# Row sums of the attention weights moved from TensorE to GpSimd, and a third PSUM bank in the ring of a two-layer graph network

## The chip, the cores and the metric

The kernel runs on one core of a Trainium2 chip. The metric is the device time of one execution in microseconds; the median of several runs is given. A profiled execution adds a trace of every instruction; its span runs from the first to the last instruction. The engines are called PE (TensorE), PEld (its weight loads), DVE (VectorE), ACT (ScalarE), POOL (GpSimd) and SP (SyncE, which issues most DMAs).

## The reference

The input `x` is (16, 1024, 256) in fp32, the adjacency `adj` (16, 1024, 1024) in int32. Two layers follow, each with a normalisation and a ReLU ahead of it and a residual around it:

```python
h = relu(layernorm(x))
# layer 0, 8 heads of 32
n = layer_norm(h, gamma1, beta1)                      # queries, keys and values are all n
s = einsum('bhqd,bhkd->bhqk', n, n) / sqrt(32)
attn = softmax(where(adj > 0, s, -inf), axis=-1)
h1 = h + einsum('bhqk,bhkd->bhqd', attn, n)
x = x + h1 + gelu(layer_norm(h1, gamma2, beta2) @ W1 + b1) @ W2 + b2
# layer 1, one head of 256
f = relu(layernorm(x))
h = f @ W
e = leaky_relu((h @ a_1).T + h @ a_2 + (h @ a_12) @ h.T, 0.2)
att = softmax(where(adj > 0, e, -9e15), axis=-1)
x = x + elu(f @ W_1 + (att @ f) @ W_2)
```

The change concerns the softmax of layer 0: its denominators, the sums of the exponentials over the keys.

## The kernel before, in words

The program holds two paths, chosen on the chip from `gamma1` and `beta1`; with these inputs `fast_path` runs. It works batch by batch (`B` = 16). In a batch, layer 0's attention is cut into 32 units: two halves of 512 queries (`qh`), two groups of four heads (`g`), eight tiles of 128 keys (`kt`). Eight units that share `qh` and `g` make a group, and there are 64 groups in all.

A unit first computes its scores (`scores`, L734): four matmuls with a contraction of 32, one for each head, into one tile `sc` of four PSUM banks (L739); the tile has one buffer only. Keys lie on the partitions, queries along the free dimension. DVE adds the mask to two heads at a time and writes an SBUF tile `e` of 128 x 1024 (L750, twice for each unit), and ACT takes the exponential in place (L751). The pool `ep` has four such tiles, two units' worth. No maximum is subtracted in this path.

`weigh` (L759) comes one unit later in PE's order, after the scores of the next unit. It has two rounds of four narrow matmuls (L770), one for each head, 32 output partitions each: the first adds exponentials times values into the bank `o`, the second multiplies the same exponentials with a tile of ones and adds up `den`, the row sums, repeated over the 32 partitions of each head. Both accumulate over the eight key tiles in the two banks of the pool `pso`. At the last key tile DVE copies `o` and ACT copies `den` to SBUF (L782). `finish` (L715) turns both by PE transposes (L721), and DVE divides (L724, L726); POOL adds the result to `h` (L728).

An fp32 matmul is two instructions for the engine, so that the profile shows 4096 where the program has 2048.

Everything else in a batch belongs to other streams: `prologue` (L663) normalises the next batch's `x`, makes the values `va` and the transposed keys `kT`; `turn_masks` (L697) loads and transposes masks; `rest` (L807) does the batch's feed-forward part (`expand`, `contract`) and layer 1 (`project`, `values`, `logits`, `soften`, `turn_weights`, `attend`). Their PE output goes through one ring of PSUM banks, the tag `ps` in the pool `psm` (L547), with two banks before. POOL does small work: the reciprocal roots of the normalisations (L652), on whose result DVE's normalising (L656) waits, the scaling of the values (L686, L687), bias and residual additions (L822, L823, L1000).

The order of the work is written by hand: each stream yields places on one scale (units of a batch), and the main loop (L1119 to L1123) always advances the stream with the lowest place. `stream_a` spreads the 32 units evenly over a batch; `stream_b` starts `rest` at 0.95 of the batch and places its pieces by their cost in microseconds, divided by `B_US` = 151. PE keeps the order in which the program issues (L1126 to L1138). On the other engines a scheduler orders the instructions. Each engine works through its own queue in order, and waits at an instruction until what it needs is done.

Of the kernel before, what the change touches and what calls it, by code (L numbers as in the profile page):

```python
# [9 lines left out]
F32 = mybir.dt.float32  # L10
# [5 lines left out]
P = 128  # L16
# [470 lines left out]
def fast_path(  # L487
# [26 lines left out]
    nc = tc.nc  # L514
    B, N, D = x.shape
    DFF = W1.shape[1]
    H, HD = 8, D // 8
    GH = 4
    NG = H // GH
    NT = N // P  # L520
    DC = D // P
    FC = DFF // P
    QW = 512
# [7 lines left out]
    pool = lambda name, bufs, **kw: ctx.enter_context(tc.tile_pool(name=name, bufs=bufs, **kw))  # L531
# [7 lines left out]
    vp = pool("vp", 2)  # L539
    midp = pool("midp", 3)  # L540
    ep = pool("ep", 4)
    lp1 = pool("lp1", 2)
    tmpp = pool("tmpp", 2)
    smallp = pool("smallp", 3)
    psc = pool("psc", 1, space=bass.MemoryType.PSUM)
    pso = pool("pso", 1, space=bass.MemoryType.PSUM)
    psm = pool("psm", 2, space=bass.MemoryType.PSUM)  # L547

    def ps_tile(shape, name, dtype=F32):
        return psm.tile(shape, dtype, tag="ps", name=name)  # L550
# [16 lines left out]
    ones = const.tile([P, HD], F32, name="ones")  # L567
# [29 lines left out]
    w2 = weight(W2, "w2")  # L597
# [112 lines left out]

    scored, summed = [], []

    def finish(b, qh, g, cs):  # L715
        h = hs[b]
        pts = []
        for n, c in cs:
            pt = ps_tile([P, TPH, P], f"pt{n}_{b}_{g}_{qh}")
            for t in range(TPH):  # L720
                nc.tensor.transpose(pt[:, t, :], c[:, t * P : (t + 1) * P], ident)  # L721
            pts.append(pt.rearrange("p t (j d) -> p t j d", d=HD))
        rl = smallp.tile([P, TPH, GH], F32, tag="rl", name=f"rl_{b}_{g}_{qh}")
        nc.vector.reciprocal(rl, pts[0][:, :, :, 0])  # L724
        ot = tmpp.tile([P, TPH, GH, HD], F32, tag="w2", bufs=3, name=f"ot_{b}_{g}_{qh}")
        nc.vector.tensor_mul(ot, pts[1], rl.unsqueeze(3).to_broadcast([P, TPH, GH, HD]))  # L726
        ho = h[:, qh * TPH : (qh + 1) * TPH, g * P : (g + 1) * P]
        nc.gpsimd.tensor_add(ho, ho, ot.rearrange("p t j d -> p t (j d)"))  # L728

    def attention(b, st):  # L730
        va, kT = st["va"], st["kT"]


        def scores(qh, g, kt):  # L734
            qs = slice(qh * QW, (qh + 1) * QW)
            sc = psc.tile([P, GH, QW], F32, tag="sc", name=f"s_{b}_{g}_{qh}_{kt}")
            for j in range(GH):
                r = slice(j * HD, (j + 1) * HD)
                nc.tensor.matmul(  # L739
                    sc[:, j, :],  # L740
                    kT[r, g, kt * P : (kt + 1) * P],
                    kT[r, g, qs],
                    start=True,
                    stop=True,
                )
            mb = st[qh][:, kt, :].unsqueeze(1).to_broadcast([P, 2, QW])
            es = []
            for i in range(2):
                e = ep.tile([P, 2, QW], F32, tag="e", name=f"e_{b}_{g}_{qh}_{kt}_{i}")
                nc.vector.tensor_tensor(e, sc[:, 2 * i : 2 * i + 2, :], mb, op=ALU.add)  # L750
                nc.scalar.activation(e, e, AF.Exp, scale=SCALE)  # L751
                es.append(e)
            return es

        acc = {}

        def weigh(qh, g, kt, es):  # L759
            if kt == 0:  # L760
                acc[g, qh] = [
                    pso.tile([P, QW], F32, tag=n, name=f"{n}_{b}_{g}_{qh}") for n in ("o", "den")
                ]
            o, den = acc[g, qh]
            for dst, lhs in (
                (o, [va[:, kt, (g * GH + j) * HD : (g * GH + j + 1) * HD] for j in range(GH)]),
                (den, [ones] * GH),
            ):
                for j in range(GH):
                    nc.tensor.matmul(  # L770
                        dst[j * HD : (j + 1) * HD, :],
                        lhs[j],
                        es[j // 2][:, j % 2, :],
                        start=(kt == 0),
                        stop=(kt == NT - 1),
                    )
            if kt < NT - 1:
                return
            cs = []
            for src, n in ((den, "ds"), (o, "os")):  # L780
                c = tmpp.tile([P, QW], F32, tag="w2", bufs=3, name=f"{n}_{b}_{g}_{qh}")
                (nc.vector.tensor_copy if n == "os" else nc.scalar.copy)(c, src)  # L782
                cs.append((n, c))
            summed.append((b, qh, g, cs))

        units = [(qh, g, kt) for qh in range(NQH) for g in range(NG) for kt in range(NT)]
        for u in units:
            es = scores(*u)
            while summed:
                finish(*summed.pop())  # L790
            while scored:
                f, args = scored.pop()
                f(*args)
            scored.append((weigh, (*u, es)))
            yield

    def close_attention():
        while scored:
            f, args = scored.pop()
            f(*args)  # L800
        yield
        while summed:
            finish(*summed.pop())

    def rest(b, tail):  # L807
# [8 lines left out]
        def prepare(c):  # L816
            ts = range(c * TPC, (c + 1) * TPC)
            mv, rs = norm_stats([h[:, t, :] for t in ts], f"c{b}_{c}")
            y = tmpp.tile([P, TPC, D], F32, tag="y", name=f"y_{b}_{c}")
            for i, t in enumerate(ts):  # L820
                normalize(y[:, i, :], h[:, t, :], mv, rs, i)
                nc.gpsimd.tensor_add(h[:, t, :], h[:, t, :], b2r)  # L822
                nc.gpsimd.tensor_add(xt[t], xt[t], h[:, t, :])  # L823
            return y
# [20 lines left out]
        def expand(c, yT):  # L845
            hid = midp.tile([P, FC, CW], F32, tag="mid", name=f"hid_{b}_{c}")
            for f0 in range(0, FC, 2):
                ph = ps_tile([P, 2, CW], f"ph_{b}_{c}_{f0}")
                for i in range(2):
                    for dc in range(DC):  # L850
                        nc.tensor.matmul(  # L851
                            ph[:, i, :],
                            w1[:, dc, (f0 + i) * P : (f0 + i + 1) * P],
                            yT[:, dc, :],
                            start=(dc == 0),
                            stop=(dc == DC - 1),
                        )
                nc.vector.tensor_tensor(  # L858
                    hid[:, f0 : f0 + 2, :],
                    ph,  # L860
                    b1c[:, f0 : f0 + 2].unsqueeze(2).to_broadcast([P, 2, CW]),
                    op=ALU.add,
                )
                yield 1.75, True
            nc.scalar.activation(hid, hid, AF.Gelu)
            return hid
# [136 lines left out]
        y = {0: prepare(0), 1: prepare(1)}  # L1003
# [1 line left out]
        yT = {0: turn(0, y[0])}  # L1005
        yield 0.5, True
        hid = {0: (yield from expand(0, yT[0]))}
        y[2] = prepare(2)
        yT[1] = turn(1, y[1])
        yield 0.5, True  # L1010
        yield from tail()
        hid[1] = yield from expand(1, yT[1])
        y[3] = prepare(3)
        yT[2] = turn(2, y[2])
# [52 lines left out]
        def tail():  # L1067
            pTs = [turn_weights(before[0], before[1], i) for i in range(2)]
            yield 0.9, True
            attend(before[0], pTs, before[2])  # L1070
            yield 4.4, True
# [6 lines left out]
    def spread(pieces, n, start, end):  # L1078
        yield start
        for i, _ in enumerate(pieces):  # L1080
            yield start + (end - start) * (i + 1) / n
# [3 lines left out]
    def stream_a():  # L1085
        for b in range(B):
            yield from spread(attention(b, states[b]), 32, b, b + 1)
        yield from spread(close_attention(), 2, B, B + 0.05)

    def stream_b():  # L1090
        tail = lambda: iter(())
        for b in range(B):
            done = 0.0
            place = b + 0.95
            yield place
            pieces = rest(b, tail)
            while True:
                try:
                    us, others = next(pieces)
                except StopIteration as end:  # L1100
                    tail = end.value
                    break
                done += us
                if others:
                    place = b + 1 + done / B_US
                yield place
        for _ in tail():
            yield B + 1
# [12 lines left out]
    while any(p is not None for p in places):  # L1121
        i = min((p, i) for i, p in enumerate(places) if p is not None)[1]
# [77 lines left out]
```

## Time and profile before

| what | before |
|---|---|
| median of 3 runs | 4816.01 us (4811.63 to 4816.24) |
| the profiled execution | 4813.6 us |
| its span | 4811.4 us |
| mean granted TensorE clock | 0.969 |
| until the first mask addition (L750) starts | 62.8 us |
| one batch between the first and the last | about 297 us |
| DMA | 192.14 MB, 12 to 13% of 16 engines |

The page lists for each engine the busy time, its share of the span, and the number of instructions. A row of a group has line, engine, operation, what is written and read, shapes and count; behind the bar stand busy time and the mean of one in ns, then the idle time of the engine just before and what ended it. Where narrow matmuls run side by side, the mean is that of one, and the busy time counts overlaps once. A row of the waits has the waiting instruction, the one it waited for, the total in us, the number of times, and the longest. A row of the timeline has the start in us, the length, engine, line and operation.

### The profile page before, as it was taken

Reading aid. Unit: us, or ns where it says so; the run is one execution under the profiler, and the core shown is the slowest. Engines: PE = TensorE matmul, PEld = TensorE weight load, DVE = VectorE, ACT = ScalarE, POOL = GpSimd, SP = SyncE. Lnnn points to the kernel's source line nnn. Section 1 sums busy time; section 2 is a strip of 40 time slices with the busy share of each in tenths; the row PEclk is TensorE's granted clock in tenths of the full one; section 3 lists DMA queues with packets and bytes.
Section 4 is the critical chain, followed back from the end, with each engine's and each line's share of the span. In section 5 each row is a group of like instructions: output and inputs, shape, how many; then the busy total and the mean of one; then the engine's idle time right before and its main releaser. Section 6 shows DMA issues by size and latency. Waiting matters only on the chain. (4 is left out here: it accounts for less than half of the span.)

```text
span 4811.4 us, 61168 instructions
## 1 busy us (share of the span) xinstructions
PE 4273.0 (89%) x24104; PEld 2316.0 (48%) x24104; DVE 2814.2 (58%) x5329; ACT 2249.5 (47%) x2941; POOL 773.0 (16%) x969
## 2 busy tenths in 40 slices
PE   5898988989899898998989989899898988989998
PEld 2354544545445454454545445454454544545456
DVE  5656655556566565665655656555565565656553
ACT  3544445444454444444444444444444444444533
POOL 3102121021210212112121121211212111021110
PEclk8999999999999999999999999999999999999999
DMA  3011111111101111011111111101111011110100
GB/s 102 27 38 46 36 42 34 44 44 32 46 29 49 40 38 40 29 50 43 39 36 34 47 44 38 37 30 47 44 38 44 23 49 42 38 42 26 37 27 27
DMA packets 133259, 192.14 MB, mean 40 GB/s; under 512 B 15586, under 2 KB 67172, under 8 KB 132964
## 3 DMA queue, kind: packets, MB, share of 16 engines
q1 hardware_dynamic: 128004, 184.60, 12.2%
q8 instruction: 192, 3.15, 0.3%
q10 hardware_dynamic: 4960, 3.55, 0.3%
q14 instruction: 103, 0.84, 0.1%
HBM read 171.32 MB, written 16.78 MB: 39 GB/s over the span
## 5 line engine op out<-in xcount | busy, mean ns | idle before, releaser
L751 ACT ACTIVATE e<-e 128x1024 f32<-128x1024 f32 x1024 | 1080.2, 1057 | 1280.0 <-DVE e L750 1255.2
L750 DVE TENSOR_TENSOR e<-s,mk 128x1024 f32<-128x1024 f32 x1024 | 1203.2, 1215 | 294.5 <-PE s L739 288.8
L739 PE MATMUL s<-kT 32*128 32x512 f32 x4096 | 598.8, 654 | 76.0 <-DVE e L750 76.0
L936 PE MATMUL lg<-fT,tT 128*128 128x512 f32 x1024 | 499.2, 631 | 109.0 <-DVE rl L724 56.5
L770 PE MATMUL o<-e,va 128*32 128x512 f32 x4096 | 567.9, 611 | 0.8 <-ACT e L751 0.7
L770 PE MATMUL den<-e,ones 128*32 128x512 f32 x4096 | 552.4, 595 | 0.0
L986 PE MATMUL pa<-gw,pT 128*128 128x256 f32 x2048 | 493.7, 396 | 26.8 <-ACT mk L709 25.8
L851 PE MATMUL ph<-yT,w 128*128 128x256 f32 x2048 | 479.9, 385 | 14.7 <-DVE yT L835 11.8
L873 PE MATMUL po<-w,hid 128*128 128x256 f32 x2048 | 467.4, 383 | 7.1 <-DVE hid L858 5.6
L986 PEld LDWEIGHTS pa<-gw,pT 128*128 128x128 f32 x2048 | 402.7, 198 | 102.7 <-ACT mk L709 34.2
L851 PEld LDWEIGHTS ph<-yT,w 128*128 128x128 f32 x2048 | 377.2, 190 | 133.2 <-issue 24.3
L873 PEld LDWEIGHTS po<-w,hid 128*128 128x128 f32 x2048 | 381.5, 190 | 98.1 <-issue 17.4
L949 DVE CUSTOM_DVE_ANT_0 e<-e,mqb 128x1024 f32<-128x1024 f32 x128 | 158.2, 1236 | 445.3 <-ACT e L943 445.2
L936 PEld LDWEIGHTS lg<-fT,tT 128*128 128x128 f32 x1024 | 193.5, 198 | 377.1 <-issue 217.9
L739 PEld LDWEIGHTS s<-kT 32*128 32x128 f32 x4096 | 167.1, 188 | 272.9 <-issue 239.4
L770 PEld LDWEIGHTS den<-e,ones 128*32 128x32 f32 x4096 | 137.1, 111 | 310.8 <-issue 310.5
L967 PE MATMUL ptp<-ident,e 128*128 128x128 f32 x1024 | 170.9, 297 | 129.0 <-ACT e L943 102.5
L858 DVE TENSOR_TENSOR hid<-ph,b1c 128x512 f32<-128x512 f32 x256 | 176.2, 688 | 171.6 <-PE ph L851 171.5
L943 ACT ACTIVATE e<-lg,gw 128x512 f32<-128x512 f32 x256 | 171.9, 683 | 200.3 <-PE lg L936 200.3
L770 PEld LDWEIGHTS o<-e,va 128*32 128x32 f32 x4096 | 83.6, 108 | 375.1 <-issue 285.3
L728 POOL TENSOR_TENSOR h<-h,ot 128x512 f32<-128x512 f32 x64 | 82.7, 1292 | 1043.8 <-DVE ot L726 907.7
L959 ACT ACTIVATE e<-e,m 128x1024 f32<-128x1024 f32 x128 | 147.0, 1149 | 195.1 <-DVE m L957 195.0
(109 smaller groups left out, 4409.0 us busy)
## 6 DMA issues: line engine op xcount, KB each, us to landing
adj_mqa<-in_adj_dram SPq DMA_DIRECT2D x256, 256.0 KB, 2.9
adj_mqb<-in_adj_dram SPq DMA_DIRECT2D x256, 256.0 KB, 2.8
xa<-in_x_dram SPq DMA_DIRECT2D x64, 256.0 KB, 2.7
xb<-in_x_dram SPq DMA_DIRECT2D x128, 128.0 KB, 2.2
out_dram<-z SPq DMA_DIRECT2D x128, 128.0 KB, 1.7
w<-in_L_gnn_W_dram ACTq DMA_DIRECT2D x2, 1024.0 KB, 9.4
wo<-in_L_gnn_W_dram ACTq DMA_DIRECT2D x2, 256.0 KB, 4.8
wl<-in_L_gnn_W_dram ACTq DMA_DIRECT2D x1, 256.0 KB
```

The lines of the kernel that those rows point to most:

```text
L739: nc.tensor.matmul(sc[:, j, :], kT[r, g, kt * P : (kt + 1) * P], kT[r, g, qs], start=True, stop=True,)
L750: nc.vector.tensor_tensor(e, sc[:, 2 * i : 2 * i + 2, :], mb, op=ALU.add)
L751: nc.scalar.activation(e, e, AF.Exp, scale=SCALE)
L770: nc.tensor.matmul(dst[j * HD : (j + 1) * HD, :], lhs[j], es[j // 2][:, j % 2, :], start=(kt == 0), stop=(kt == NT - 1),)
L851: nc.tensor.matmul(ph[:, i, :], w1[:, dc, (f0 + i) * P : (f0 + i + 1) * P], yT[:, dc, :], start=(dc == 0), stop=(dc == DC - 1),)
L858: nc.vector.tensor_tensor(hid[:, f0 : f0 + 2, :], ph, b1c[:, f0 : f0 + 2].unsqueeze(2).to_broadcast([P, 2, CW]), op=ALU.add,)
L873: nc.tensor.matmul(po, hid[:, f, i * P : (i + 1) * P], w2[:, f, :], start=(f == 0), stop=(f == FC - 1),)
L936: nc.tensor.matmul(lg, tT[:, dc, t * P : (t + 1) * P], fT[:, dc, c * QW : (c + 1) * QW], start=(dc == 0), stop=(dc == DC - 1),)
L943: nc.scalar.activation(e[:, c * QW : (c + 1) * QW], lg, AF.Identity, bias=gw[:, t, D : D + 1])
L949: nc.vector.tensor_tensor_reduce(e, e, mq, 1.0, -3.0e38, op0=ALU.add, op1=ALU.max, accum_out=m1[:, 0:1])
L967: nc.tensor.transpose(pt[:, i, :], e[:, k * P : (k + 1) * P], ident)
L986: nc.tensor.matmul(pa, pTs[kt // TPH][:, kt % TPH, :], gw[:, kt, :D], start=(kt == 0), stop=(kt == NT - 1),)
```

## The change

The row sums are no longer a matmul at every key tile. `add_up` adds the exponentials of the key tiles on POOL into two SBUF tiles `acc` of 128 x 1024 (new pool `accp`, one buffer for each): at `kt` = 0 it only keeps the tiles, at `kt` = 1 it adds the first two, later it adds to `acc`. That makes two additions of 128 x 1024 in seven of eight units. `total` then does one round of four matmuls with the ones for each group, on the sums, into a bank of the ring `ps`, and ACT copies it out. `pso` keeps one bank (`o`), and `psm` gets a third.

`go_on` runs once for each unit: it finishes one group, totals another, weighs the unit before. A group's end is therefore spread over three units instead of two, `close_attention` has three pieces, `prepare(2)` of `rest` is moved behind the tail of the batch before, and batch 0 has a piece of 5.3 us in the place of the missing tail, which moves its places alone.

```diff
--- before.py
+++ after.py
@@ -539,12 +539,13 @@
     vp = pool("vp", 2)
     midp = pool("midp", 3)
     ep = pool("ep", 4)
+    accp = pool("accp", 1)
     lp1 = pool("lp1", 2)
     tmpp = pool("tmpp", 2)
     smallp = pool("smallp", 3)
     psc = pool("psc", 1, space=bass.MemoryType.PSUM)
     pso = pool("pso", 1, space=bass.MemoryType.PSUM)
-    psm = pool("psm", 2, space=bass.MemoryType.PSUM)
+    psm = pool("psm", 3, space=bass.MemoryType.PSUM)
 
     def ps_tile(shape, name, dtype=F32):
         return psm.tile(shape, dtype, tag="ps", name=name)
@@ -710,12 +711,23 @@
 
 
 
-    scored, summed = [], []
-
-    def finish(b, qh, g, cs):
+    scored, weighed, totalled = [], [], []
+
+    def total(b, qh, g, os, acc):
+
+        den = ps_tile([P, QW], f"den_{b}_{g}_{qh}")
+        for j in range(GH):
+            nc.tensor.matmul(
+                den[j * HD : (j + 1) * HD, :], ones, acc[j // 2][:, j % 2, :], start=True, stop=True
+            )
+        ds = tmpp.tile([P, QW], F32, tag="w2", bufs=3, name=f"ds_{b}_{g}_{qh}")
+        nc.scalar.copy(ds, den)
+        totalled.append((b, qh, g, ds, os))
+
+    def finish(b, qh, g, ds, os):
         h = hs[b]
         pts = []
-        for n, c in cs:
+        for n, c in (("ds", ds), ("os", os)):
             pt = ps_tile([P, TPH, P], f"pt{n}_{b}_{g}_{qh}")
             for t in range(TPH):
                 nc.tensor.transpose(pt[:, t, :], c[:, t * P : (t + 1) * P], ident)
@@ -755,52 +767,59 @@
         acc = {}
 
 
-
         def weigh(qh, g, kt, es):
             if kt == 0:
-                acc[g, qh] = [
-                    pso.tile([P, QW], F32, tag=n, name=f"{n}_{b}_{g}_{qh}") for n in ("o", "den")
+                acc[g, qh] = pso.tile([P, QW], F32, tag="o", name=f"o_{b}_{g}_{qh}")
+            o = acc[g, qh]
+            for j in range(GH):
+                nc.tensor.matmul(
+                    o[j * HD : (j + 1) * HD, :],
+                    va[:, kt, (g * GH + j) * HD : (g * GH + j + 1) * HD],
+                    es[j // 2][:, j % 2, :],
+                    start=(kt == 0),
+                    stop=(kt == NT - 1),
+                )
+            if kt == NT - 1:
+                c = tmpp.tile([P, QW], F32, tag="w2", bufs=3, name=f"os_{b}_{g}_{qh}")
+                nc.vector.tensor_copy(c, o)
+                weighed.append((b, qh, g, c, sums.pop((g, qh))))
+
+        sums, first = {}, {}
+
+
+        def add_up(qh, g, kt, es):
+            if kt == 0:
+                first[g, qh] = es
+                return
+            if kt == 1:
+                sums[g, qh] = [
+                    accp.tile([P, 2, QW], F32, tag=f"acc{i}", name=f"acc_{b}_{g}_{qh}_{i}")
+                    for i in range(2)
                 ]
-            o, den = acc[g, qh]
-            for dst, lhs in (
-                (o, [va[:, kt, (g * GH + j) * HD : (g * GH + j + 1) * HD] for j in range(GH)]),
-                (den, [ones] * GH),
-            ):
-                for j in range(GH):
-                    nc.tensor.matmul(
-                        dst[j * HD : (j + 1) * HD, :],
-                        lhs[j],
-                        es[j // 2][:, j % 2, :],
-                        start=(kt == 0),
-                        stop=(kt == NT - 1),
-                    )
-            if kt < NT - 1:
-                return
-            cs = []
-            for src, n in ((den, "ds"), (o, "os")):
-                c = tmpp.tile([P, QW], F32, tag="w2", bufs=3, name=f"{n}_{b}_{g}_{qh}")
-                (nc.vector.tensor_copy if n == "os" else nc.scalar.copy)(c, src)
-                cs.append((n, c))
-            summed.append((b, qh, g, cs))
+            for i, a in enumerate(sums[g, qh]):
+                nc.gpsimd.tensor_add(a, first[g, qh][i] if kt == 1 else a, es[i])
 
         units = [(qh, g, kt) for qh in range(NQH) for g in range(NG) for kt in range(NT)]
         for u in units:
             es = scores(*u)
-            while summed:
-                finish(*summed.pop())
-            while scored:
-                f, args = scored.pop()
-                f(*args)
+            go_on()
             scored.append((weigh, (*u, es)))
+            add_up(*u, es)
             yield
 
-    def close_attention():
-        while scored:
+    def go_on():
+        if totalled:
+            finish(*totalled.pop())
+        if weighed:
+            total(*weighed.pop())
+        if scored:
             f, args = scored.pop()
             f(*args)
-        yield
-        while summed:
-            finish(*summed.pop())
+
+    def close_attention():
+        for _ in range(3):
+            go_on()
+            yield
 
 
 
@@ -1005,10 +1024,10 @@
         yT = {0: turn(0, y[0])}
         yield 0.5, True
         hid = {0: (yield from expand(0, yT[0]))}
-        y[2] = prepare(2)
         yT[1] = turn(1, y[1])
         yield 0.5, True
         yield from tail()
+        y[2] = prepare(2)
         hid[1] = yield from expand(1, yT[1])
         y[3] = prepare(3)
         yT[2] = turn(2, y[2])
@@ -1085,10 +1104,10 @@
     def stream_a():
         for b in range(B):
             yield from spread(attention(b, states[b]), 32, b, b + 1)
-        yield from spread(close_attention(), 2, B, B + 0.05)
+        yield from spread(close_attention(), 3, B, B + 0.05)
 
     def stream_b():
-        tail = lambda: iter(())
+        tail = lambda: iter([(5.3, True)])
         for b in range(B):
             done = 0.0
             place = b + 0.95
```

## The prediction

> **What bounds the kernel now.** I read the page first: busy times, the slices, the groups of instructions.
>
> ```profile
> PE 4273.0 (89%) x24104; PEld 2316.0 (48%) x24104; DVE 2814.2 (58%) x5329; ACT 2249.5 (47%) x2941; POOL 773.0 (16%) x969
> ...
> PE   5898988989899898998989989899898988989998
> ...
> L750 DVE TENSOR_TENSOR e<-s,mk 128x1024 f32<-128x1024 f32 x1024 | 1203.2, 1215 | 294.5 <-PE s L739 288.8
> ...
> L770 PE MATMUL o<-e,va 128*32 128x512 f32 x4096 | 567.9, 611 | 0.8 <-ACT e L751 0.7
> L770 PE MATMUL den<-e,ones 128*32 128x512 f32 x4096 | 552.4, 595 | 0.0
> ```
>
> TensorE (PE) is busy 89%, in every slice alike; the others have room. The two L770 rows are the weighted sum `o` and the row sum `den`: 1024 rounds of four narrow matmuls each, two rounds per unit (a unit is one head group, half the queries, one key tile; 16 x 32 = 512 units). PE's idle time is 4811.4 - 4273.0 = 538 us; PE's waits, longest first, tell where:
>
> ```profile
> PE ptp L967 <- ACT e L943: 102.5, 110, 4.6
> PE s L739 <- DVE e L750: 76.0, 80, 4.7
> PE lg L936 <- DVE rl L724: 56.5, 28, 2.3
> PE lg L936 <- ACT kT L694: 51.0, 28, 2.5
> PE pg L923 <- ACT fT L898: 43.0, 28, 3.6
> PE pf L976 <- ACT kT L694: 37.1, 14, 3.0
> ```
>
> Most are not data: `lg` doesn't use `rl` or `kT`. They are waits for one of the two banks of the ring `ps`, until its last reader is done. Added up over the list, such waits are some 340 us. Only 76 us are waits for the mask addition on VectorE (DVE).
>
> What a round of `den` costs is read from the timeline of PE, one unit:
>
> ```profile
> 2026.16 1.06 PE L770 MATMUL o<-e,va 128*32 128x512 f32 x8
> 2027.04 1.04 PE L770 MATMUL den<-e,ones 128*32 128x512 f32 x8
> 2028.02 0.66 PE L831 MATMUL pty<-ident,y 128*128 128x128 f32 x4
> ```
>
> `den` starts 0.88 us after `o` (median of all such pairs 0.88), the next work 0.97 us after `den`. Bars overlap, so a unit without `den` is 0.88 us shorter, not 1.04.
>
> [...] A stretch of the timeline:
>
> ```profile
> 3080.58 1.32 DVE L949 CUSTOM_DVE_ANT_0 e<-e,mqb 128x1024 f32<-128x1024 f32 x1 [0.35 <-ACT e L943]
> 3080.89 1.59 POOL L823 TENSOR_TENSOR xb<-xb,h 128x256 f32<-128x256 f32 x1
> ...
> 3081.94 1.62 DVE L953 SCALAR_TENSOR_TENSOR e<-e 128x1024 f32<-128x1024 f32 x1
> ...
> 3082.44 1.70 POOL L822 TENSOR_TENSOR h<-h,b2r 128x256 f32<-128x256 f32 x1
> ```
>
> L823 takes 0.73 us by median, here 1.59: it ends after L949. L953 takes 1.22 alone, here 1.62: it waits for L823. L822 then waits for L953. They alternate, one whole instruction each. By class, DVE operations that start under a busy POOL: L559 421 ns becomes 1353, L999 424 becomes 836, L953 1224 becomes 1632. L750 reads one input from PSUM, and stays at 1216 against 1209: free of the lock.
>
> [...] Here 256 elements take 0.73 us (L1000) and 512 take 1.265 (L728); [...] the slope of the two rows of this trace gives the same.
>
> [...] eight matmuls of 592 ns fill 1.04 us. [...] The pools held 4 (scores) + 2 (`o`, `den`) + 2 (ring); now 4 + 1 + 3.
>
> **The change part by part.**
>
> *`den` leaves PE.* 512 x 0.88 = 451 us removed; one sum per group comes back, 64 x 0.97 = 62. PE gains 388 us, all on the engine that sets the end.
>
> *Third bank.* Of the 340 us of bank waits I take 200: a wait for the tile two back becomes one for the tile three back, with one more PE tile (1 to 2 us) of cover, against mean waits of 0.9 to 2.7 us. Bounds 100 and 300. The sum tile now also passes through the ring, 64 times.
>
> *Additions on POOL.* 7 x 2 x 64 = 896 of 2.35 us: 2105 us. POOL goes from 773 to some 2880, plus lock waits (160 additions would begin inside a contending DVE operation: 85 us). It is 62% of 4800: not the bound by sum. But three things follow.
>
> 1. The lock. DVE has 2176 contending operations (L559 512, L656 512, L650 256, and L949, L953, L954, L957, L996, L998, L999 128 each). I laid the additions on the trace of before, each pair from the ends of its two exponentials (the first ends as the unit's second L750 does, the second 1.15 us later, by median), 2.35 us each. 669 of the 2176 start inside such a window; 393 windows are hit, and the first hit of each waits 514 us together. The other 276 move on and can meet the second addition, since they alternate: half of 2.35 us each, 324 us. Of this some 90 us is there already.
> 2. POOL is in order. 256 reciprocal roots (L652) stand among the additions, and DVE's next instruction waits for each (`y` and `ft` waited 94.5 and 50 us for POOL). They find an addition running 44% of the time, for 1.2 us on average: 135 us. Behind a waiting addition stand also `va` (L687), which PE's `ptk` needs, `z` (L1000), ahead of the output DMA on SP's queue, and the `h` update (L728), for which `st_c` waits; these I put at nothing, since POOL has 38% idle and the next use is mostly a unit away; without that cover `st_c` alone would cost 64 x 2.35 = 150 us.
> 3. Exponential tiles. Four buffers, now also held by the addition. A unit's tiles are wanted back two units on, some 15 us later, and the additions end 6 us after the unit's second L750: nothing, except where units follow each other in 3.7 us (three of 32).
>
> DVE's delay is then 514 + 324 - 90 + 135 = 883 us, 1.7 us per unit. What reaches PE? Next in line is `s`: it needs L750 of the unit before, since there is one score buffer. From the start of each `s` and the end of the L750 before it I took the slack of each unit: median 4.7 us, 83 of 511 under 0.3. With units 0.88 us shorter and DVE 1.8 us later, the shortfalls sum to 264 us, against 13 now: 250. With 3.8 us later they would be 711, with none 62. For later evacuations of ring tiles (L858, L880, L993), with three banks, I add 30. New PE wait: 280 us.
>
> *Order.* A group is finished in three steps over three units; `prepare(2)` comes after the tail of the batch before, and batch 0's places shift by 5.3 of 151. The same instructions, covered by the PE work of the other streams, which is laid out by the same plan; uncovered, one unit's delay at the very end, under 10 us. The copy of `den` on ScalarE (64 x 0.57 us) stays.
>
> **Sum.** 4811.4 - 388 - 200 + 280 = 4503 us of span. The profiled execution took 4813.6, 2.2 over its span, and the median of the runs, 4816.0, lies 2.4 above that: 4508 us.
>
> **Rivals.**
>
> *B, DVE's idle time takes it all.* DVE is idle 41%. If the blocked operations have slack, only the 50 us of the shorter units are left, and some evacuation waits: 4811 - 388 - 200 + 55 + 5 = 4283. For it: median slack 4.7 us is two additions long. Against: 83 units have none.
>
> *C, slower: the lock makes DVE the bound.* The place is the stretch right behind the two L750 of a unit: there the two additions start, and there DVE wants to do its other work. In the instruction order of the changed kernel 368 of the 448 units with additions have two or more contending operations before the next L750. If each loses both additions, less some 0.9 us of free work, 368 x 3.8 = 1400 us, DVE is busy 2814 - 90 + 1400 = 4124. To this come waits that no backlog fills: before the first L750 32 us, in the last 178 us 108, for POOL's roots 165 + 135, for ScalarE (L960, L998) 158, and half of L949's 445: 820. 4944 + 5, about 4945 us. It decides once DVE loses some 3.5 us per unit, since the 588 us that PE gained are then waited away (the shortfalls above). For it: the alternation is in the trace, and the heavy L949 and L953 stand in that stretch. Against: in the trace only 669 of 2176 fall into a window; the rest wait for PE's results and come later.
>
> *D, both cancel*, within 0.2%: the time at which between A and C the delays eat 588 us exactly.
>
> That the row sums stay on PE can be excluded: the instruction order has 64 sums left.
>
> **Numbers.** A (4508; own range 4380 to 4640) 0.50, B 0.20, C 0.25, D 0.05. Within 0.2% is about what a measurement of this kernel can't tell from no change. Faster 0.70, same 0.05, slower 0.25. The range 4260 to 4930 leaves out the lower third of B and half of C.
>
> **What would show it.** The `den` row at about 512 matmuls and 64 us; 896 POOL additions of 2.35 us or more; PE busy near 3890. Right on the lock: L559, L656, L953 longer by a microsecond, L750 at 1.21, DVE busy near 3560. Right on the bank: `lg <- rl` and `lg <- kT` nearly gone. For A, `s <- e L750` among PE's waits at about 260 us; for B under 100; for C DVE over 85% and this wait over 600. An addition of 3 us or more, or roots queued behind several additions, would make me wrong upwards.

## The result, and the profile after

The changed kernel takes 5012.5 us (5005.2 to 5019.3, four runs), against 4814.4 for the kernel before in the same session: ratio 1.041, 95% interval 1.039 to 1.043. It is slower. The forecast was 4508, the range 4260 to 4930. The profiled execution took 5007.0 us, its span 5005.2.

The page after begins with busy times and slices; then come three rows of the groups: the additions, the mask addition of the scores, and the first half of VectorE's mask conversions (L560, the old L559):

```profile
PE 4073.1 (81%) x20520; PEld 2271.3 (45%) x20520; DVE 3428.1 (68%) x5329; ACT 2207.7 (44%) x2941; POOL 2958.8 (59%) x1865
...
PEclk8798998999989999999998999999898998999999
...
L800 POOL TENSOR_TENSOR acc<-acc,e 128x1024 f32<-128x1024 f32 x768 | 1861.7, 2443 | 823.6 <-ACT e L763 817.1
...
L762 DVE TENSOR_TENSOR e<-s,mk 128x1024 f32<-128x1024 f32 x1024 | 1206.9, 1213 | 217.8 <-PE s L751 209.6
...
L560 DVE TENSOR_SCALAR mqa<-adj_mqa 128x512 bf16<-128x512 int32 x256 | 317.4, 1275 | 11.4 <-DMA adj_mqa<-in_adj_dram 6.4
```

The last of them had this row before:

```profile
L559 DVE TENSOR_SCALAR mqa<-adj_mqa 128x512 bf16<-128x512 int32 x256 | 118.1, 497 | 8.7 <-DMA adj_mqa<-in_adj_dram 6.3 <-PE ptm L708 1.7
```

The sums left PE as announced (20520 matmuls instead of 24104). The additions take 2.44 us each with their waits. L762, the mask addition of the scores, is as fast as before; this half of the mask conversions went from 497 ns on average to 1275. PE's busy time fell by 200 us, not by 388, and its idle time rose from 538 to 932. Its longest waits:

```profile
PE s L751 <- DVE e L762: 277.9, 131, 9.6
PE ptp L986 <- ACT e L962: 170.7, 75, 6.2
PE pg L942 <- ACT fT L917: 77.1, 14, 6.2
PE ptk L694 <- ACT kT L695: 70.1, 15, 4.9
PE pa L1005 <- DVE rl L736: 56.8, 15, 3.8
PE ph L870 <- DVE yT L854: 52.2, 16, 4.6
```

One wait in full, from the timeline of all engines:

```profile
2001.82 4.85 POOL L800 TENSOR_TENSOR acc<-acc,e 128x1024 f32<-128x1024 f32 x2 [1.88 <-ACT e L763]
2002.03 4.92 DVE L560 TENSOR_SCALAR mqa<-adj_mqa 128x512 bf16<-128x512 int32 x2
...
2007.83 0.43 DVE L560 TENSOR_SCALAR mqb<-adj_mqb 128x512 bf16<-128x512 int32 x1 [0.89 <-DMA adj_mqb<-in_adj_dram]
2008.17 0.48 DVE L1012 SCALAR_TENSOR_TENSOR z<-pa,l,z 128x256 f32<-128x256 f32 x1
2008.71 0.30 PEld L955 LDWEIGHTS lg<-fT,tT 128*128 128x128 f32 x2 [3.65 <-DVE z L1012]
2008.71 3.56 PE L955 MATMUL lg<-fT,tT 128*128 128x512 f32 x4 [3.41 <-DVE z L1012]
```

Two mask conversions, which take 0.42 us each when nothing stands in their way, start beside two additions and take 4.92 us together. That one holds up the other is what is called the lock here: in the trace after, L560 takes 418 ns on average where GpSimd is idle at its start and 1715 where it is busy, L972 (the old L953) 1222 and 2887, L762 1214 and 1212. The mask load behind them came late, because its buffer did, and VectorE waited 0.89 us for it. L1012, which reads a bank of the ring, is queued behind all of that, and PE stands still for 3.41 us at a matmul that only wants the bank. Then it pays once more. The work after the wait, and `lg` twenty microseconds later, in a table of busy times by window (the eighth column is the granted clock):

```profile
2008.70:2012.30 3.60, 3.59 (x5) 1.53 (x6) 1.43 (x5) 0.95 (x3) 0.73 (x1) 0.54 0.56 182
2028.40:2032.00 3.60, 3.60 (x13) 1.64 (x10) 2.21 (x2) 2.41 (x3) 3.52 (x5) 1.00 0.00 1
```

At a clock of 0.54 the four matmuls of `lg` above take 3.56 us; at 1.00, from 2028.38 on, eight of them take 3.70. Half clock follows a wait of 3.41 us here; the last section shows that shorter idling was enough, too. Over the whole execution the trace has half clock for 304 us before and 817 us after; the mean fell from 0.969 to 0.919.

### The profile page after: what moved, and what is told of

It is laid out like the page before. It is cut to its first block, busy times and chain, and to the rows that moved or that the text cites. A ratio compares the mean times of both kernels' runs of the same rounds, so it can differ in the third digit from the quotient of the medians.

```text
span 5005.2 us, 55833 instructions
## 1 busy us (share of the span) xinstructions
PE 4073.1 (81%) x20520; PEld 2271.3 (45%) x20520; DVE 3428.1 (68%) x5329; ACT 2207.7 (44%) x2941; POOL 2958.8 (59%) x1865
## 4 chain that ended last, share of the span: by engine, by line
DVE 36%; PE 32%; ACT 11%; POOL 9%; issue 7%; DMA 4%; ACTq 0%; DVEq 0%; POOLq 0%; SPq 0%
DVE e L762 12%; PE pa L1005 6%; PE po L892 6%; ACT e L763 5%; PE s L751 5%; POOL acc L800 4%; DVE e L972 4%; DMA adj_mqb<-in_adj_dram 4%; DVE mqa L560 4%; PE ph L870 3%; PE lg L955 3%; PE o L775 3%; DVE e L968 3%; ACT e L962 2%; PE pg L942 2%
## 5 line engine op out<-in xcount | busy, mean ns | idle before, releaser
L800 POOL TENSOR_TENSOR acc<-acc,e 128x1024 f32<-128x1024 f32 x768 | 1861.7, 2443 | 823.6 <-ACT e L763 817.1
L762 DVE TENSOR_TENSOR e<-s,mk 128x1024 f32<-128x1024 f32 x1024 | 1206.9, 1213 | 217.8 <-PE s L751 209.6
L751 PE MATMUL s<-kT 32*128 32x512 f32 x4096 | 660.0, 716 | 277.9 <-DVE e L762 277.9
L775 PE MATMUL o<-e,va 128*32 128x512 f32 x4096 | 639.9, 661 | 0.6 <-ACT e L763 0.6
L800 POOL TENSOR_TENSOR acc<-e,e 128x1024 f32<-128x1024 f32 x128 | 334.5, 2636 | 494.6 <-ACT e L763 268.1
L955 PE MATMUL lg<-fT,tT 128*128 128x512 f32 x1024 | 521.0, 655 | 47.2 <-DVE z L1012 39.8
L870 PE MATMUL ph<-yT,w 128*128 128x256 f32 x2048 | 504.4, 399 | 53.4 <-DVE yT L854 52.2
L1005 PEld LDWEIGHTS pa<-gw,pT 128*128 128x128 f32 x2048 | 413.2, 203 | 195.0 <-DVE rl L736 62.8
L870 PEld LDWEIGHTS ph<-yT,w 128*128 128x128 f32 x2048 | 396.8, 199 | 176.7 <-DVE yT L854 56.8
L968 DVE CUSTOM_DVE_ANT_0 e<-e,mqb 128x1024 f32<-128x1024 f32 x128 | 211.3, 1651 | 346.4 <-ACT e L962 346.3
L978 ACT ACTIVATE e<-e,m 128x1024 f32<-128x1024 f32 x128 | 147.0, 1149 | 480.6 <-DVE m L976 480.6
L560 DVE TENSOR_SCALAR mqa<-adj_mqa 128x512 bf16<-128x512 int32 x256 | 317.4, 1275 | 11.4 <-DMA adj_mqa<-in_adj_dram 6.4
L972 DVE SCALAR_TENSOR_TENSOR e<-e 128x1024 f32<-128x1024 f32 x128 | 259.7, 2029 | 3.9
```

What stands on the lines that cost most here:

```text
L560: nc.vector.tensor_scalar(m[:, c : c + QW], a, 0.0, NEG, op0=ALU.is_le, op1=ALU.mult)
L751: nc.tensor.matmul(sc[:, j, :], kT[r, g, kt * P : (kt + 1) * P], kT[r, g, qs], start=True, stop=True,)
L775: nc.tensor.matmul(o[j * HD : (j + 1) * HD, :], va[:, kt, (g * GH + j) * HD : (g * GH + j + 1) * HD], es[j // 2][:, j % 2, :], start=(kt = ...
L800: nc.gpsimd.tensor_add(a, first[g, qh][i] if kt == 1 else a, es[i])
L870: nc.tensor.matmul(ph[:, i, :], w1[:, dc, (f0 + i) * P : (f0 + i + 1) * P], yT[:, dc, :], start=(dc == 0), stop=(dc == DC - 1),)
L955: nc.tensor.matmul(lg, tT[:, dc, t * P : (t + 1) * P], fT[:, dc, c * QW : (c + 1) * QW], start=(dc == 0), stop=(dc == DC - 1),)
```

## The experiments

The theory after the result was the *lock*: additions and VectorE's operations exclude each other, VectorE comes late everywhere, PE waits and loses clock. The rivals were the *queue* (GpSimd is full, whatever it does), and the *cover*, with the new order (PE's gain turns into waits once the row sums, which filled them, are gone). All times are medians, compared with the kernel before in the same session, 4805 to 4814 us. Where an edit is shown in part, `...` stands for the rest. In the runs whose denominators are partial or fixed, the copy of `den` also adds 1; the copy then takes 0.67 to 0.68 us instead of 0.57 or 0.58, 64 times.

**Few additions.** The first of seven additions stays.

```diff
...
+            if kt > 1:
+                return
             for i, a in enumerate(sums[g, qh]):
-                nc.gpsimd.tensor_add(a, first[g, qh][i] if kt == 1 else a, es[i])
+                nc.gpsimd.tensor_add(a, first[g, qh][i], es[i])
```

> The changed kernel with only the first of the seven additions of each group (128 of 896 additions left, so the denominators are partial sums, with 1 added in their copy). Lock theory: VectorE loses its waits for the additions (VectorE busy about 2850 us), TensorE's waits fall to about 450 us, the granted clock comes back to 0.97: 4300 to 4450 us. Queue theory: the same. Order theory (the thinner cover after the sums left TensorE, and the new order of finishing a group, make the waits): no better than 4850.

Measured: 4522 us, ratio 0.939 (0.936 to 0.942). So 768 additions cost 490 us. It is 70 us above what the lock theory allowed, with a clock of 0.947 and 591 us idle: something else remains in PE's waits. The page line, and the wait of the scores:

```profile
PE 3928.4 (87%) x20520; PEld 2220.6 (49%) x20520; DVE 2882.4 (64%) x5329; ACT 2212.5 (49%) x2941; POOL 1106.1 (24%) x1097
```

```profile
PE s L751 <- DVE e L762: 131.5, 88, 9.4
```

**The queue without the lock.**

```diff
...
+                    for k in range(3 + i):
+                        nc.gpsimd.tensor_tensor(
+                            roots[g, qh][:, 2 * kt + i, k, :], es[i][:, k % 2, 2 * k : 2 * k + 2], mhalf[:, :2], op=ALU.pow
+                        )
```

> As the run with few additions, but each left-out addition is replaced by three or four tiny power operations (128 x 2 elements, about 0.70 us each in the traces), on the same exponential tiles and at the same places of GpSimd's queue: GpSimd is as long occupied (2.1 and 2.8 us), holds the exponential tiles as long, but reads SBUF hardly at all. The denominators are partial sums. Lock theory: within 60 us of the run with few additions. Queue theory (VectorE and TensorE wait because GpSimd's queue is full): 4900 to 5010 us, with VectorE's waits for rs and TensorE's for kT as in the changed kernel.

Measured: 4673 us, ratio 0.972 (0.969 to 0.974). GpSimd was as full as in the changed kernel, as the row shows:

```profile
L806 POOL TENSOR_TENSOR roots<-e,mhalf 128x2 f32<-128x2 f32 x2688 | 1883.8, 735 | 646.0 <-ACT e L763 644.7
...
L560 DVE TENSOR_SCALAR mqa<-adj_mqa 128x512 bf16<-128x512 int32 x256 | 145.7, 605 | 9.3 <-DMA adj_mqa<-in_adj_dram 5.8 <-PE ptm L709 3.2
```

Busy 1884 us against 1862 for the additions. The mask conversion takes 605 ns instead of 1275; in the run with few additions it takes 540, so that the tiny operations themselves add little at the lock. Added up over VectorE's 2176 operations that the prediction counted as contending, the time beyond their free one is about 195 us here, 180 with few additions, and 740 in the changed kernel. Neither theory had it alone: of the 490 us the occupied queue costs some 151 (4673 - 4522) and the long reading of SBUF, 128x1024 each time instead of 128x2, 340 (5012 - 4673). What the 151 consist of, the order of GpSimd's queue or the exponential tiles held longer, was not taken apart.

**Two banks.** `psm` with 2 instead of 3.

```diff
-    psm = pool("psm", 3, space=bass.MemoryType.PSUM)
+    psm = pool("psm", 2, space=bass.MemoryType.PSUM)
```

> The changed kernel with two banks in the ring instead of three. If the third bank is worth the 200 us that the prediction gave it: about 5200 us. If its gain is lost in the other waits: 5010 to 5060 us.

Measured: 5348 us, ratio 1.112 (1.110 to 1.114). The third bank is worth 336 us here, more than the prediction gave it.

**Additions on top of the kernel before.** `add_up` and its tiles put into the kernel before, called after each unit; nothing taken out.

```diff
...
+            for i, a in enumerate(sums[g, qh]):
+                nc.gpsimd.tensor_add(a, first[g, qh][i] if kt == 1 else a, es[i])
...
```

> The kernel before, with its row sums on TensorE as they were and two banks, and with the 896 additions on GpSimd besides, whose sums nobody reads. Lock theory: the additions alone cost what the run with few additions gains over the changed kernel, some 500 to 600 us, less what the row-sum matmuls give in cover and in a clock that stays up: 5100 to 5300 us. If the additions are harmless and the rearrangement is at fault: 4830 us or less.

Measured: 5296 us, ratio 1.101 (1.099 to 1.103): the additions alone cost 484 us, within the old order. The run with two banks has the additions as well, its row sums mostly off PE, and the new order: it takes 5348. Under the additions, then, 388 us less work on PE gained nothing that the new order didn't take.

**Few additions, two banks.** Both edits above.

> The run with few additions (4522 us), with two banks in the ring instead of three; the denominators are again partial sums with 1 added. This is the row sums leaving TensorE, alone. By the prediction's steps (388 us of TensorE work gone, the bank worth 200): about 4720 us. Cover theory (TensorE waited less before because the row-sum matmuls filled the time in which banks were read out, so that their removal turns into waits): the bank is worth as much as under the additions, 336 us, and this run is at 4800 to 4860 us, no better than the kernel before.

Measured: 4843 us, ratio 1.008 (1.006 to 1.009). The bank is worth 321 us here as well. With two banks the rearrangement gains nothing, as the cover theory had it; but it has 128 additions and a new order in it, which two later runs take apart.

**Masks on ScalarE.**

```diff
-            nc.vector.tensor_scalar(m[:, c : c + QW], a, 0.0, NEG, op0=ALU.is_le, op1=ALU.mult)
+            nc.scalar.activation(m[:, c : c + QW], a, AF.Identity, bias=negc[:, 0:1], scale=-NEG)
...
```

> The changed kernel with the conversion of the masks (512 instructions, the class with the largest waits at the lock, 293 of 741 us) on ScalarE instead of VectorE. Lock theory: 340 us of the time were lost for 741 us of VectorE waits, so 293 of them are worth some 130 us, and 220 us of work less on VectorE some 40 more: 4830 to 4900 us. If VectorE's waits don't matter, or ScalarE with some 320 us more becomes late: 5010 us or more.

Measured: 4777 us, ratio 0.994 (0.992 to 0.996), 236 us under the changed kernel and just under the kernel before. More came back than either number said.

**Sums on VectorE.**

```diff
-                nc.gpsimd.tensor_add(a, first[g, qh][i] if kt == 1 else a, es[i])
+                nc.vector.tensor_add(a, first[g, qh][i] if kt == 1 else a, es[i])
```

> The changed kernel with the 896 additions on VectorE, about 1.2 us each, 1090 us more on VectorE (about 3850 us busy), no lock and no GpSimd queue. If it is the lock's waits at bad moments that cost: 4750 to 4950 us. If it is only the sum of VectorE's time that counts (the additions on GpSimd lengthened it by 614 us): 5050 us or more.

Measured: 4623 us, ratio 0.962 (0.961 to 0.964), with nothing left out of the computation: 3.8% faster than the kernel before. VectorE is busy 3793 us, more than the 3428 of the changed kernel, and yet it is 389 us faster. The sum of VectorE's time is not what counts. Its row:

```profile
L800 DVE TENSOR_TENSOR acc<-acc,e 128x1024 f32<-128x1024 f32 x768 | 938.2, 1235 | 38.7 <-ACT e L763 31.6
```

**Sums split.** One of the two additions on each engine.

```diff
-                nc.gpsimd.tensor_add(a, first[g, qh][i] if kt == 1 else a, es[i])
+                (nc.vector if i else nc.gpsimd).tensor_add(a, first[g, qh][i] if kt == 1 else a, es[i])
```

> The changed kernel with one of the two additions of each unit on VectorE and one on GpSimd. Lock theory: half of the lock's and the queue's cost (490 / 2 = 245 us) goes, and 550 us of work on VectorE come: 4800 to 5000 us. If the sum of VectorE's time counts (550 + about 310 of waits): about 5100 us.

Measured: 5015 us, ratio 1.042 (1.040 to 1.044), as slow as with all of them on GpSimd. Neither number fits. The rows point to why:

```profile
L800 POOL TENSOR_TENSOR acc<-acc,e 128x1024 f32<-128x1024 f32 x384 | 921.9, 2401 | 1286.2 <-ACT e L763 1284.7 <-DMA out_dram<-z 1.6
L800 DVE TENSOR_TENSOR acc<-acc,e 128x1024 f32<-128x1024 f32 x384 | 784.2, 2042 | 265.1 <-ACT e L763 262.8
```

VectorE's own addition takes 2042 ns on average beside GpSimd's of the same unit, instead of 1235 with all of them on VectorE: it stands at the lock, too. Over its 448 additions that is, by estimate, some 360 us; with about 280 us that the other operations lose at the lock it makes 640, hardly less than the 740 of the changed kernel. The lock theory had been applied without this class, which only the experiment created. No run takes this wait out alone.

**Both repairs.** Sums on VectorE, masks on ScalarE.

> Additions on VectorE (4623 us) and the mask conversion on ScalarE. VectorE then is busy some 3570 us instead of 3793. If its load is what keeps this version above the run with few additions (4522): 4530 to 4580 us. If the lock was the only thing that the masks' move repaired in the changed kernel: 4620 us, or more where ScalarE becomes late.

Measured: 4625 us, ratio 0.962 (0.960 to 0.963). No more than the sums on VectorE alone. With the additions gone from GpSimd, a move that takes some 145 us off VectorE is worth nothing.

**The control.** Masks on ScalarE in the kernel before.

> The control for the move of the masks: the kernel before with the mask conversion on ScalarE, nothing else. Lock theory: there is nearly no lock to repair and TensorE is the bound, so 4790 to 4830 us, where the same move won 236 us in the changed kernel. If unloading VectorE is worth the same everywhere: about 4600 us.

Measured: 4862 us, ratio 1.012 (1.010 to 1.014). Slower by 57 us, outside both numbers, where the same edit gained 236 in the changed kernel. Together with the last run: what it repaired there came from the additions on GpSimd. That it was the lock, and not GpSimd's full queue, is argued from the row of L560 (1275 ns instead of 497) and not shown by these two runs. Why it costs 57 here was not tried; PE's waits for `kT`, which ScalarE copies, went from 51 to 85 us at `lg`.

**Row sums once, in the old order.**

```diff
...
+                if once and kt < NT - 1:
+                    continue
...
-                        start=(kt == 0),
+                        start=(kt == 0 or once),
...
```

> The kernel before, in its own order and with two banks, with the row-sum matmuls in the last key tile of each group alone, started there (the denominators are sums over one key tile, with 1 added). TensorE loses 7 of 8 rounds, 395 us of work by their distance, and nothing else changes. By the prediction's step: about 4430 us. Cover theory (the rounds filled time in which TensorE would have waited, and kept the clock up): 4700 to 4830 us. If it comes near 4450, then it is the new order of finishing a group that ate the gain.

Measured: 4637 us, ratio 0.964 (0.962 to 0.966). Between the two numbers: 395 us of work off the bounding engine are worth 168. PE's page line and its first waits:

```profile
PE 3946.7 (85%) x20520; PEld 2214.9 (48%) x20520; DVE 2807.9 (60%) x5329; ACT 2245.1 (48%) x2941; POOL 771.2 (17%) x969
```

```profile
PE s L739 <- DVE e L750: 135.2, 79, 5.7
PE ptp L972 <- ACT e L948: 127.7, 111, 5.4
PE lg L941 <- DVE rl L724: 81.6, 28, 3.2
```

These waits have grown from 76.0, 102.5 and 56.5 in the kernel before; others fell, such as that of `lg` for `kT`, from 51.0 to 23.4. Idle time is 699 us, 161 more, and half clock 454 us, 150 more. Of the 395 us of work, then, 161 came back as waits; PE's busy time fell by 326 only, so that by this sum some 69 came back in matmuls that take longer; the span of this profile is 165 us shorter. What the row sums cost they partly gave back as cover.

**No additions, two banks.** The changed kernel with two banks and with fixed tiles of ones as sums.

```diff
...
-            for i, a in enumerate(sums[g, qh]):
-                nc.gpsimd.tensor_add(a, first[g, qh][i] if kt == 1 else a, es[i])
+                sums[g, qh] = fixed
...
```

> The run with few additions and two banks (4843 us), without the 128 additions that were left in it: the sums are fixed tiles of ones, so the denominators are constants. It differs from the kernel before with its row sums only once (4637 us) only in the order of finishing a group and in the ring, through which the sum tile now passes. If the new order and the sum tile in the ring made the 206 us between those two: 4820 us or more. If the 128 additions made them (1/7 of the 490 us that the others cost is 70): 4770 us; if the additions alone did it: 4640 us.

Measured: 4735 us, ratio 0.984 (0.983 to 0.986), between the numbers. So the new order with the sum tile in the ring costs 98 us (4735 - 4637), the 128 first additions 108 (4843 - 4735). An addition that begins a group is dearer than a later one (0.84 us each against 0.64), within what two differences of this kind can tell.

## Why the prediction was wrong, point by point

The runs make a chain from the kernel before to the changed one. Each row is one step; the second bundles all that changed in the order, with the sum tile's way through the ring:

| step | time after it, us | difference | the prediction's term |
|---|---|---|---|
| kernel before (in the session of the next row) | 4805 | | |
| row sums once for each group, old order | 4637 | -168 | -388 |
| new order of finishing, sum tile in the ring | 4735 | +98 | 0 |
| 128 first additions | 4843 | +108 | part of +280 |
| third bank | 4522 | -321 | -200 |
| GpSimd's queue occupied as by the other 768 | 4673 | +151 | part of +280 |
| those 768 additions, reading SBUF | 5012 | +340 | part of +280 |

What a step is worth depends on where it stands. All 896 additions cost 484 us in the old order, 613 in the new order with two banks (5348 - 4735), and 599 along this chain.

*What held.* The addition was priced at 2.35 us (the slope of the two rows of before, 1.265 - 0.73 = 0.535 us for 256 elements, gives 1.265 + 2 x 0.535 = 2.335) and has a median of 2.37. The lock was there, and L750 free of it. Which of VectorE's operations contend was the author's estimate; the trace after shows it for nine of the ten lines. Means where GpSimd is idle at the start, and where it is busy, in ns: L560, L972 and L762 as above; L657 409 and 787, L651 157 and 768, L968 1225 and 1823, L973 149 and 677, L1015 291 and 1161, L1017 294 and 874, L1018 425 and 816. For the tenth, L976 (the old L957, 128 of the 2176), it is not shown: 148 and 154. L1012, counted as free, has 479 and 483. VectorE's operations at the lock took 741 us more than their free time, against 838 forecast, part of which was there before. By class the waits were smaller than the microsecond announced: 0.57 us on average for L560, 0.80 for L972, 0.12 for L657 (the old L656). Roots behind additions cost little: VectorE's waits for `rs` of `y` and `ft` rose from 144.5 to 197.5 us. The exponential tiles cost nothing, as forecast: VectorE waited 5.9 us for one that an addition held. The two signs for the bank came, too (`lg` for `rl` 1.0 us, for `kT` 6.4), but other bank waits took their place, as the list above shows. The two signs that were to announce an error upwards, additions of 3 us or roots behind several additions, did not come: the additions take 2.44 us on average, and no wait of `y` or `ft` for a root was longer than 3.0 us.

*The step that failed* is "What reaches PE?", behind the three points on the additions, with its 280 us: 250 for `s`, 30 for the later evacuations, and nothing for the clock. Additions cost 108 + 151 + 340 = 599 us. Where it went is seen between the run with few additions and the changed kernel, which differ by 768 additions and 486 us of span:

| part of PE's time | few additions | changed kernel | difference |
|---|---|---|---|
| wait of `s` for L762 | 131.5 | 277.9 | +146 |
| all other idle time | 459 | 654 | +195 |
| busy, with the same 20520 matmuls | 3928.4 | 4073.1 | +145 |

The wait of `s` was forecast at about 260 us and came out at 277.9, but this agreement is partly luck: 131.5 of it is there with few additions, and the 768 others add 146. The rest of the damage is 340 us, where the forecast had 30. The other evacuations are late because VectorE works through its queue in order (in the trace after, its 332 instructions of a batch come in one order through 14 batches on end, none starting over 0.1 us before the end of the one ahead; GpSimd's 116 do the same, within 0.2 us): what is late at the lock delays every bank reader behind it, as L1012 above. And ScalarE follows VectorE: its `en` (L1016) waited 364.0 us for `en` of L1015, 274.7 before, its L978 480.6 instead of 195.0 for the maximum `m`, and the copies `kT` and `fT`, for which PE waits, stand in the same queue. PE hardly waited for an addition itself: 13.2 us, by its weight loads.

*What had no term* is the clock, the last row of the table: 0.947 with few additions, 0.919 in the changed kernel, paid in matmuls that take longer after a wait. Every wait of 2 us or more was costed at its own length.

*The second step that failed* is the `den` term: "PE gains 388 us, all on the engine that sets the end". The work was sized rightly, but the term took the work for the gain. The run in the old order gives 168: the other 220 us were cover for waits and for the clock. Such a count was made for the exponential tiles, the roots and the order, not for the matmuls removed.

*The third bank* went the other way, 321 instead of 200, outside the bounds of 100 and 300. In the run with few additions and two banks PE waits 69.5 us at `ph` for `hid`, 64.9 at `ph` for `rl` and 64.0 at `pf` for `rl`; with three banks none of these is left, and in the run with the row sums once, in the old order with two banks, they are under 10 us each. So the bank also repairs waits that came with the new order, and the two terms can't be added freely.

*The order of finishing*, costed at nothing, costs 98 us with two banks. Which part of it does (the step over three units, the sum tile in the ring, `prepare(2)` behind the tail) was not tried, nor its price with three banks. The four errors, 319 for the additions, 220 for `den`, 98 for the order and 121 the other way for the bank, make up the distance to the forecast (504 us) but for 12 us.

*Rival C*, slower, with a chance of 0.25, was the right side, but not by its mechanism: VectorE did not become the bound. It is busy 68%, and with 82% (sums on VectorE) the kernel is faster. Also the first batch, in which attention runs alone, went from 141 to 187 us: there GpSimd is busy 158 us of the 189 around it, close to being the bound, and the prediction didn't look at this stretch by itself. A small point on a reading: the 1353 ns of L559 under a busy POOL rest on few instances; over all 24 that start so, the mean is 1253.

## What to carry to other kernels

Work moved to an idle engine is not free if its operations and those of an engine that stands between the bounding engine and its buffers hold each other up, as the additions did L560 (1275 ns instead of 497): price not its busy time, but which of the neighbour's operations it holds up and who is queued behind them. Work removed from the bounding engine is worth its length less the waits that it covered: look at what stands behind the removed instructions before the gain is booked. Here the same additions on VectorE, where each takes half as long (1235 ns instead of 2443) and the first half of L560 takes 425 ns (1275), make the kernel 3.8% faster than before and 7.8% faster than the changed one, although VectorE is then the fuller engine. Where that gain comes from is a further lesson: along the chain, taking the row sums off PE and the new order together gave 70 us, the bank that `den` left free 321. No run has the sums on VectorE with two banks, so this is not shown for that kernel.

## What the runs showed of the hardware that was not expected

Half clock followed less idling than the wait of 3.41 us above. The traces have the granted clock in pieces of 3.41 us and multiples of it, all but the last. Past the first 100 us, PE had been idle for 2.1 us by median of the 3.4 us ahead of a half-clock stretch in the kernel before, 1.6 at least; 2.7 and 1.8 in the changed one. Idle stretches of PE that began at full clock can be sorted by whether half clock set in before 3.4 us had gone by after their end. In the changed kernel it did for none of the 63 stretches of 1 to 2 us, 38 of 63 of 2 to 3 us, 48 of 56 of 3 to 4 us, and all 67 longer ones; in the kernel before it also did for 16 of 75 of 1 to 2 us. So waits of 2 to 3 us often cost clock already, and no stretch of 3.4 us without any work on PE was needed.

Two engines that add the same pair of tiles side by side were no faster (5015 us) than one doing all of it alone (5012 on GpSimd).
